# Moving the degree stores, the biases, the g row products and two Wv sums in the opening of a two-layer graph kernel

## The chip, the cores and the metric

The kernel runs on one core of one Trainium2 chip. The metric is the device time of one execution in microseconds (us); for a version it is the median of several runs. Everything is float32. The engines are PE (TensorE), DVE (VectorE), ACT (ScalarE), POOL (GpSimd) and SP (SyncE, which here only issues DMAs).

## The reference

64 graphs of 256 nodes with 512 features each, and a dense 256x256 adjacency per graph. Layer 0 is an attention masked by the adjacency, layer 1 a graph convolution, both on a layer-normed, rectified input and both with a residual:

```
h = relu(layernorm(x))
q, k, v = h @ Wq.T + bq, h @ Wk.T + bk, h @ Wv.T + bv
w = adj * exp(q @ k.T);  w = w / w.sum(-1)
x = x + w @ v
h = relu(layernorm(x))
A = adj + I;  d = A.sum(-1) ** -0.5
x = x + (A * d[:, None] * d[None, :]) @ (h @ W + b)
```

## The kernel before

**Tiling.** The graphs go in 32 pairs, p = 0 to 31. A pair's features are four blocks of 128 nodes x 512 (`TB` = 4), its adjacency four of 128 x 256. Every matrix product is done by a scheme of seven half-size products instead of eight, which needs sums and differences of the operands' quarters (`left_sums`, `right_steps`, `weight_steps`, suffixes S1 to S4). The stages of a pair are g (query-key product with the merged matrix M = Wq.T Wk, `query_stage`), v (values), s (scores and softmax), o (weights times values), l (neighbours' sum) and w (times W1); g1 is product 1 of stage g, and so on. PE runs the products in an order written out as a string of such tokens (L1113, L1144, L1153), one behind the other (`in_order`, L289). `work` lists the calls that follow each token on the other engines.

**Rounds.** The first `run` (L1112) does stages g, v and s of pair 0. Then round p does o, l, w of pair p and g, v, s of pair p + 1. Ahead of the first run lies the opening: PE runs ten products of a constant (`run_in`, L202), then M from Wq's and Wk's rows (`merge_query_key`, L208, 32 products of 128x256, two passes each), then 16 turns of pair 0's normed features (`transpose_features`, L410; ACT copies them out of PSUM at L419). PSUM has six buffers for all products.

**The other opening work.** `measure(p)` (L333) takes means and variances of the features of pair p on VectorE (L308, L309), and GpSimd turns them into scale and offset (L298, L300, L317, L319: `irs`, `irr`, `nm`, `nb`). `norm_features(p)` (L336) then applies them on ScalarE (L325). `degrees(p)` (L350) sums the adjacency's rows on VectorE (L353), takes the root on GpSimd and stores the 512 degrees from SP to DRAM, an element of 4 bytes at a time (`dflat`, L356). `spread_degrees(p)` (L359) loads them back as a row for all partitions (`drow`, L362); `weigh_degrees(p)` (L365, line L372) uses that row. `bias_products` (L248) computes bq.bk (`bb`, `bs`) and, through `weighted_rows` (L236), the rows g = sum of bq * Wk's rows: four multiplies on ScalarE and three adds on GpSimd (L243, L245). A second call (L1091) does c = sum of bk * Wq's rows, in the buffers with the tags "hbS" and "U2". `bias_terms` (L256, products `pc_gb`) and `query_row` (L266, product `c_all`) use them. `find_terms` (L393, line L398) needs `c_all`; `corner` (L643, line L646) reads stage g's products out of PSUM; `find_query_sums` (L478) is lines L436 to L439, `turn_blocks` (L404) line L408, `move` (L421) line L430; L785 is the first read of stage s's bank 1. Wv's quarters are turned at L273, and its four sums are L181 to L184 on VectorE; W1's four sums are the same lines on GpSimd.

**Order.** Within an engine instructions run in the order in which they stand; `tc.issue_after(x)` says that what is made within it stands behind x. [...] The biases bq and bk are loaded from GpSimd's queue (L131, L132), each as 128 x 4 elements of 4 bytes. Wk's three parts go from SP's queue and Wq's from ACT's (L136); behind Wk's on SP's queue follow pair 0's features (L101) and adjacency (L106), pair 1's features, Wv (L145), and then `load_the_rest` (L149), in whose middle `spread_degrees(0)` stands (L159). `degrees(0)` stores its row ahead of all of `load_the_rest`. `degrees(1)` follows token g2 (L1122), and Wv's sums follow g2 and g3.

Of the kernel before, what the change touches and what calls it, by code (L numbers as in the profile page):

```python
# [9 lines left out]
F32 = mybir.dt.float32  # L10
# [6 lines left out]
def kernel(  # L17
# [35 lines left out]
    nc = tc.nc  # L53
    P = 128
    B, N, D = x.shape
# [7 lines left out]
    DC = D // P  # L63
# [9 lines left out]
    p1 = ctx.enter_context(tc.tile_pool(name="p1", bufs=1))  # L73
# [7 lines left out]
    sub, add, mult = ALU.subtract, ALU.add, ALU.mult  # L81
# [7 lines left out]
    def load_x(p):  # L89

        x_tiles[p] = xp.tile([P, TB, D], F32, tag="x", name=f"x_{p}")
        for g in range(G):
            nc.sync.dma_start(of_graph(x_tiles[p], g), in_dram(x, p, g))
# [3 lines left out]
    def load_features(p):  # L97

        feats[p] = hp.tile([P, TB, D], F32, tag="h", name=f"h_a{p}")
        for g in range(G):  # L100
            nc.sync.dma_start(of_graph(feats[p], g), in_dram(x, p, g))  # L101
# [19 lines left out]
    wk_rows = p1.tile([P, DC, D], F32, tag="gT", name="wk_rows")  # L121
    wq_w1 = p1.tile([P, 7, 2, HD], F32, tag="yS", name="wq_w1")
    wq_rows = wq_w1[:, 0:DC].rearrange("p c h d -> p c (h d)")
# [4 lines left out]
    b_qk = const.tile([P, 2, DC], F32, tag="b_qk", name="b_qk")  # L128
    bqT, bkT = b_qk[:, 0], b_qk[:, 1]
    b1_all = const.tile([P, D], F32, tag="b1", name="b1_all")  # L130
    nc.gpsimd.dma_start(bqT, bq.rearrange("(c p) -> p c", p=P))  # L131
    nc.gpsimd.dma_start(bkT, bk.rearrange("(c p) -> p c", p=P))  # L132
    for first, count, half in ((0, 2, 0), (2, 2, 0), (0, 4, 1)):
        rows, cols = slice(first * P, (first + count) * P), ts(half, HD)
        for eng, tile_, w in ((nc.sync, wk_rows, wk), (nc.scalar, wq_rows, wq)):
            eng.dma_start(  # L136
                tile_[:, first : first + count, cols],
                w[rows, cols].rearrange("(c p) d -> p c d", p=P),
            )
    load_features(0)  # L140
    load_a(0)
    load_features(1)
# [6 lines left out]
    def load_the_rest():  # L149
        w1_view = w1.rearrange("(j t p) (i f) -> i j p t f", p=P, t=2, f=HD)  # L150
        nc.sync.dma_start(w1_set[:, A11], w1_view[0, 0])
        nc.sync.dma_start(w1_set[:, A12], w1_view[0, 1])
        nc.sync.dma_start(w1_21, w1_view[1, 0])
        nc.sync.dma_start(w1_set[:, A22], w1_view[1, 1])
        load_a(1)
        load_features(2)
        load_blocks(0)
        load_x(0)
        spread_degrees(0)  # L159
        load_x(1)  # L160
        nc.sync.dma_start(b1_all, b1.partition_broadcast(P))
# [10 lines left out]
    v_set = const.tile([P, 7, 2, HD], F32, tag="wv", name="v_set")  # L172
# [6 lines left out]
    def weight_steps(w, w21, eng=nc.vector):  # L179
        return [  # L180
            lambda: eng.tensor_tensor(w[:, S1], w21, w[:, A22], add),  # L181
            lambda: eng.tensor_tensor(w[:, S2], w[:, S1], w[:, A11], sub),
            lambda: eng.tensor_tensor(w[:, S3], w[:, A11], w21, sub),
            lambda: eng.tensor_tensor(w[:, S4], w[:, A12], w[:, S2], sub),  # L184
        ]
# [16 lines left out]
    def run_in():  # L202

        pm = ps_m.tile([P, P], F32, tag="pm", name="pm_run_in")
        for _ in range(10):
            in_order(pm, ones_sq, ones_sq, start=True, stop=True)

    def merge_query_key(behind_rows, behind_turns):  # L208


        m21 = p1.tile([P, 2, HD], F32, tag="A1", name="m21")
        for half, dcs in ((0, (0, 1)), (1, (0, 1)), (0, (2, 3)), (1, (2, 3))):
            pm = {
                dc: ps_m.tile([P, HD], F32, tag="pm", name=f"pm_mT_{dc}_{half}") for dc in dcs
            }
            for ocs in ((0, 1), (2, 3)):
                for dc in dcs:
                    for oc in ocs:
                        in_order(
                            pm[dc],  # L220
                            wq_rows[:, oc, ts(dc, P)],
                            wk_rows[:, oc, ts(half, HD)],
                            start=oc == 0,
                            stop=oc == DC - 1,
                        )
            for dc in dcs:
                to = half_of(m_set, m21, half, dc // 2)[:, dc % 2, :]
                if dc < 2 or half == 0:
                    with tc.issue_after(behind_rows):
                        behind_rows = nc.scalar.copy(to, pm[dc]).ins  # L230
                else:
                    with tc.issue_after(behind_turns):
                        behind_turns = nc.vector.tensor_copy(to, pm[dc]).ins
        return weight_steps(m_set, m21), behind_rows, behind_turns

    def weighted_rows(w, b, three, one, behind=None):  # L236

        more = p1.tile([P, DC - 1, D], F32, tag=three, name=f"wr_{three}")
        acc = p1.tile([P, D], F32, tag=one, name=f"wr_{one}")
        parts_ = [acc] + [more[:, i] for i in range(DC - 1)]  # L240
        for oc in range(DC):
            with tc.issue_after(behind) if behind else ExitStack():
                last = nc.scalar.mul(parts_[oc], w[:, oc, :], b[:, oc : oc + 1])  # L243
        for oc in range(1, DC):
            added = nc.gpsimd.tensor_tensor(acc, acc, parts_[oc], add)  # L245
        return acc, last.ins, added.ins

    def bias_products():  # L248
        bb = const.tile([P, DC], F32, tag="bb", name="bb")
        nc.vector.tensor_tensor(bb, bqT, bkT, mult)  # L250
        bs = const.tile([P, 1], F32, tag="bs", name="bs")
        nc.vector.tensor_reduce(bs, bb, AX.X, add)
        return bs, *weighted_rows(wk_rows, bqT, "vS", "A0")


    def bias_terms(bs, g_rows):  # L256
# [9 lines left out]
    def query_row(c_rows):  # L266
        in_order(c_all, ones_sq, c_rows, start=True, stop=True)

    v21 = p1.tile([P, 2, HD], F32, tag="wS", name="v21")

    def value_weight_steps():
# [9 lines left out]
    norms, deg, ds, terms, blocks, hTs, parts, second, sides = ({} for _ in range(9))  # L281
    flats, gTs, query_parts, weights, row_sums, turned, wTs, weight_parts, value_parts, aTs = (
        {} for _ in range(10)
    )

    measured, offsets = [], []
# [8 lines left out]
    def inverse_root(src, plus, name, tag="ir_r"):  # L295

        s = sm.tile([P, TB], F32, tag="ir_s", name=f"irs_{name}")
        nc.gpsimd.tensor_scalar(s, src, plus, None, add)  # L298
        r = sm.tile([P, TB], F32, tag=tag, name=f"irr_{name}")
        nc.gpsimd.tensor_tensor(r, s, minus_half, ALU.pow)  # L300
        return r
# [48 lines left out]
    def degrees(p):  # L350

        sums = sm.tile([P, TB], F32, tag="deg", name=f"deg_{p}")
        measured.append(nc.vector.tensor_reduce(sums, a_tiles[p], AX.X, add).ins)  # L353
        d = inverse_root(sums, 1.0, f"d{p}", "d")
        flats[p] = dr.tile([NT], F32, tag="drow", name=f"dflat_{p}")
        nc.sync.dma_start(flats[p].rearrange("(t p) -> p t", p=P), d)  # L356
        deg[p] = d, None

    def spread_degrees(p):  # L359

        row = p1.tile([P, NT], F32, tag="drow", name=f"drow_{p}")
        nc.sync.dma_start(row, flats[p].partition_broadcast(P))  # L362
        deg[p] = deg[p][0], row
# [719 lines left out]
        return work  # L1083

    run_in()
    bs, g_rows, last_act, last_pool = bias_products()
    with tc.issue_after(last_pool):
        measure(0)
    first_offsets = offsets[-1]
    with tc.issue_after(first_offsets):  # L1090
        c_rows, turned_rows, last_pool = weighted_rows(wq_rows, bkT, "hbS", "U2", last_act)  # L1091
    with tc.issue_after(measured[-1]), tc.issue_after(last_pool):
        degrees(0)
        with tc.issue_after(measured[-1]):
            measure(1)
    m_steps, last_act, last_dve = merge_query_key(turned_rows, measured[-1])
    load_the_rest()
    with tc.issue_after(last_act):
        norm_features(0)
# [4 lines left out]
        + value_weight_steps(),  # L1104
        last_dve,
    )
    v_steps = weight_steps(v_set, v21)
    with tc.issue_after(offsets[-1]):
        weight_sums(w1_set, w1_21, nc.gpsimd)
    behind = ExitStack()  # L1110
# [8 lines left out]
        {  # L1119
            "g1": [(norm_features, 1)],  # L1120
            "g6": [(lambda p: bias_terms(bs, g_rows), 0)],
            "g2": [(lambda p: query_row(c_rows), 0), (degrees, 1), (lambda p: [s() for s in v_steps[:2]], 0)],  # L1122
            "g7": [(find_terms, 0)],
            "g3": [(find_query_sums, 0), (turn_blocks, 1), (lambda p: [s() for s in v_steps[2:]], 0)],
            "v5": [(move, 1, 0, 6, nc.gpsimd)],
            "v6": [(move, 1, 6, 8)],
            "s1": [(move, 1, 8, 12)],
# [2 lines left out]
            "v2": [(move_weights, 0, 0, 8)],  # L1130
            "v3": [
                (turn_adjacency, 0),
                (weigh_degrees, 0),
                (spread_degrees, 1),
                (measure, 2),
# [14 lines left out]
    p = NP - 2  # L1150
# [74 lines left out]
```

## Time and profile before

| | us |
|---|---|
| median of the runs | 1806.53 |
| lowest and highest of the runs | 1805.68, 1808.04 |
| the profiled execution | 1807.14 |
| its span, from the first to the last instruction | 1805.0 |
| PE busy in the span | 1784.7 |
| VectorE, ScalarE, GpSimd busy | 1327.4, 1162.8, 1204.8 |
| granted TensorE clock, mean over the span | 0.998 |

All times in what follows count from the span's start. A line of the timeline has the start, the duration, the engine, the line of the kernel, the operation, what is written and read, and in brackets the engine's idle time before it and what ended that. "SPq" is a DMA issue by SP. A line of the waits has the total in us, the number of times and the longest. A matmul in float32 counts as two in the profile.

### The profile page before, as it was taken

Reading aid. Unit: us, or ns where it says so; the run is one execution under the profiler, and the core shown is the slowest. Engines: PE = TensorE matmul, PEld = TensorE weight load, DVE = VectorE, ACT = ScalarE, POOL = GpSimd, SP = SyncE. Lnnn points to the kernel's source line nnn. Section 1 sums busy time; section 2 is a strip of 40 time slices with the busy share of each in tenths; the row PEclk is TensorE's granted clock in tenths of the full one; section 3 lists DMA queues with packets and bytes.
Section 4 is the critical chain, followed back from the end, with each engine's and each line's share of the span. In section 5 each row is a group of like instructions: output and inputs, shape, how many; then the busy total and the mean of one; then the engine's idle time right before and its main releaser. Section 6 shows DMA issues by size and latency. Waiting matters only on the chain.

```text
span 1805.0 us, 29095 instructions
## 1 busy us (share of the span) xinstructions
PE 1784.7 (99%) x9968; PEld 1614.2 (89%) x9968; DVE 1327.4 (74%) x3054; ACT 1162.8 (64%) x2318; POOL 1204.8 (67%) x1326
## 2 busy tenths in 40 slices
PE   8999999999999999999999999999999999999998
PEld 7889988999989999989999889999899999899987
DVE  5877878777777677777678786777776777776676
ACT  4676667766677666677666767666776666776542
POOL 4467676676666676666676766776666766667763
PEclk9999999999999999999999999999999999999999
DMA  8634443544533444444444434444434444333331
GB/s 194 151 88 100 112 106 83 117 80 108 120 87 98 113 86 111 111 83 112 100 98 113 96 90 119 77 111 113 92 101 106 94 111 112 83 111 71 65 76 47
DMA packets 253603, 182.58 MB, mean 101 GB/s; under 512 B 163728, under 2 KB 184208, under 8 KB 253456
## 3 DMA queue, kind: packets, MB, share of 16 engines
q1 hardware_dynamic: 235424, 146.11, 28.7%
q0 software_dynamic: 16960, 33.56, 13.6%
q8 instruction: 80, 1.31, 0.3%
q10 hardware_dynamic: 1072, 1.05, 0.2%
q14 instruction: 67, 0.55, 0.1%
HBM read 147.07 MB, written 33.62 MB: 100 GB/s over the span
## 4 chain that ended last, share of the span: by engine, by line
PE 93%; DVE 3%; DMA 1%; ACT 1%; POOL 1%; issue 1%; SPq 0%; DVEq 0%; ACTq 0%; POOLq 0%
PE pm_g L292 21%; PE pm_w L292 21%; PE pm_v L292 20%; PE pm_s L292 10%; PE pm_o L292 10%; PE pm_l L292 10%; DMA a<-in_adj_dram 1%; DMA wk_rows<-in_L_gnn_Wk_w_dram 0%; ACT h_b L325 0%; DVE st_b L308 0%; POOL wr_U L245 0%; DVE e L774 0%; POOL wr_A L245 0%; ACT e L764 0%; DVE x L838 0%
## 5 line engine op out<-in xcount | busy, mean ns | idle before, releaser
L292 PE MATMUL pm_w<-w_set,yS 128*128 128x256 f32 x1792 | 399.1, 380 | 1.7 <-ACT U_w L922 1.3
L292 PEld LDWEIGHTS pm_w<-w_set,yS 128*128 128x128 f32 x1792 | 335.4, 190 | 45.3 <-issue 1.4
L430 ACT COPY hT<-hq 32x512 f32<-32x512 f32 x490 | 301.9, 616 | 10.2 <-DVE hq L408 2.7
L292 PE MATMUL pm_g<-hT,m_set 128*128 128x256 f32 x1024 | 239.0, 381 | 5.9 <-DVE gT L646 5.0
L292 PE MATMUL pm_v<-v_set,hT 128*128 128x256 f32 x1024 | 237.0, 379 | 0.1
L913 DVE SCALAR_TENSOR_TENSOR x<-pm_w,irr_d,x 128x256 f32<-128x256 f32 x256 | 110.8, 474 | 164.7 <-POOL x L923 114.8
L292 PEld LDWEIGHTS pm_g<-hT,m_set 128*128 128x128 f32 x1024 | 195.3, 191 | 34.0 <-DVE gT L646 5.4
L292 PEld LDWEIGHTS pm_v<-v_set,hT 128*128 128x128 f32 x1024 | 192.0, 190 | 25.6 <-DVE v L725 0.9
L512 ACT COPY wT<-eq 32x256 f32<-32x256 f32 x504 | 202.3, 401 | 5.9
L292 PE MATMUL pm_v<-v_set,hS 128*128 128x256 f32 x768 | 176.6, 380 | 0.0
L292 PE MATMUL pm_g<-hS,m_set 128*128 128x256 f32 x768 | 176.3, 379 | 0.2 <-DVE hS L449 0.2
L292 PEld LDWEIGHTS pm_g<-hS,m_set 128*128 128x128 f32 x768 | 145.8, 190 | 20.4 <-DVE hS L449 0.6
L292 PEld LDWEIGHTS pm_v<-v_set,hS 128*128 128x128 f32 x768 | 144.0, 191 | 18.5
L838 POOL TENSOR_TENSOR x<-x,A_o 128x512 f32<-128x512 f32 x62 | 82.0, 1324 | 111.4 <-ACT A_o L836 108.2
L764 ACT ACTIVATE e<-e,ks 128x128 f32<-128x128 f32 x192 | 66.5, 395 | 83.9 <-DVE e L802 43.5
L946 POOL TENSOR_TENSOR yS<-yS,U_l 128x512 f32<-128x512 f32 x32 | 40.7, 1272 | 118.6 <-DVE yS L945 114.8
L325 ACT ACTIVATE h_b<-x,nb_b,rs_b 128x512 f32<-128x512 f32 x128 | 93.7, 802 | 18.8 <-POOL nb_b L319 18.8
L292 PE MATMUL pm_l<-aT,h_b 128*128 128x128 f32 x776 | 102.9, 275 | 2.5 <-DVE U_l L936 2.2
L292 PE MATMUL pm_s<-hT,gT 128*128 128x128 f32 x768 | 101.3, 275 | 3.5 <-DVE e L785 3.5
L292 PEld LDWEIGHTS pm_s<-hT,gT 128*128 128x128 f32 x768 | 97.9, 192 | 7.4 <-DVE e L785 4.3
L832 DVE TENSOR_TENSOR x<-pm_o,x 128x512 f32<-128x512 f32 x128 | 87.6, 686 | 17.7 <-PE pm_o L292 17.1
L436 POOL TENSOR_TENSOR wS<-wT 128x256 f32<-128x256 f32 x32 | 23.4, 730 | 115.5 <-ACT wT L512 115.5
(182 smaller groups left out, 3938.2 us busy)
## 6 DMA issues: line engine op xcount, KB each, us to landing
h_a<-in_x_dram SPq DMA_DIRECT2D x64, 512.0 KB, 7.1
x<-in_x_dram SPq DMA_DIRECT2D x64, 512.0 KB, 4.4
x<-in_L_gnn_Wv_b_dram POOLq DMA_DIRECT2D x32, 1024.0 KB, 10.2
out_dram<-x SPq DMA_DIRECT2D x62, 512.0 KB, 3.5
a<-in_adj_dram SPq DMA_DIRECT2D x64, 256.0 KB, 2.9
aq<-in_adj_dram SPq DMA_DIRECT2D x128, 128.0 KB, 3.6
drow<-dflat SPq DMA_DIRECT2D x32, 256.0 KB, 5.9
wv_blocks<-in_L_gnn_Wv_w_dram SPq DMA_DIRECT2D x4, 256.0 KB, 6.8
```

The lines of the kernel that those rows point to most:

```text
L292: last_product[0] = nc.tensor.matmul(*args, **kwargs).ins
L325: nc.scalar.activation(h[:, t, :], xt[:, t, :], AF.Relu, bias=nb[:, t : t + 1], scale=rd[:, t : t + 1],)
L430: copy(dst[j * Q : (j + 1) * Q, i], src[i * Q : (i + 1) * Q, j])
L436: eng.tensor_tensor(s1, a21, a22, add)
L512: copy(dst[j * Q : (j + 1) * Q, i], src[i * Q : (i + 1) * Q, j])
L764: nc.scalar.activation(block(qb, kb)[:, g], scores[:, g], AF.Exp, bias=terms[p][:, t : t + 1])
L832: read(nc.vector.tensor_tensor(block(n, i), bank, block(n, i), add))
L838: read(eng.tensor_tensor(block(n, i), block(n, i), more, add))
L913: nc.vector.scalar_tensor_tensor(to, bank[:, r, :], factor(n, r), to, mult, add)
L946: read(nc.gpsimd.tensor_tensor(t2, b22, t["part"], sub))
```

## The change

- The loads of bq and bk leave GpSimd's queue: bq goes to SP's queue behind Wk's three parts and ahead of the features, bk to ACT's queue behind Wq's three parts.
- `run_in` has eight products instead of ten.
- g is computed on VectorE alone (one multiply, three multiply-and-adds of 128x512). c alone is left to `weighted_rows`; its buffers are now "hbS" and "aS".
- `degrees` no longer stores for pair 0; a new function `flatten` does, and for pair 0 it is called in `load_the_rest` behind `load_x(0)`.
- `degrees(1)` moves from token g2 to token v3, the last of the first run, behind `turn_adjacency(0)`.
- Wv's sums S1 and S2 stay on VectorE, S3 and S4 go to GpSimd; all four are made behind g2.

```diff
-    nc.gpsimd.dma_start(bqT, bq.rearrange("(c p) -> p c", p=P))
-    nc.gpsimd.dma_start(bkT, bk.rearrange("(c p) -> p c", p=P))
     for first, count, half in ((0, 2, 0), (2, 2, 0), (0, 4, 1)):
...
+    nc.sync.dma_start(bqT, bq.rearrange("(c p) -> p c", p=P))
+    nc.scalar.dma_start(bkT, bk.rearrange("(c p) -> p c", p=P))
     load_features(0)
...
         load_x(0)
+        flatten(0)
         spread_degrees(0)
         load_x(1)
...
-        for _ in range(10):
+        for _ in range(8):
...
-    def weighted_rows(w, b, three, one, behind=None):
+    def weighted_rows(w, b):
-        more = p1.tile([P, DC - 1, D], F32, tag=three, name=f"wr_{three}")
-        acc = p1.tile([P, D], F32, tag=one, name=f"wr_{one}")
+        more = p1.tile([P, DC - 1, D], F32, tag="hbS", name="wr_more")
+        acc = p1.tile([P, D], F32, tag="aS", name="wr_acc")
...
-        return bs, *weighted_rows(wk_rows, bqT, "vS", "A0")
+        g_rows = p1.tile([P, D], F32, tag="A0", name="g_rows")
+        nc.vector.tensor_scalar(g_rows, wk_rows[:, 0, :], bqT[:, 0:1], None, mult)
+        for oc in range(1, DC):
+            last = nc.vector.scalar_tensor_tensor(
+                g_rows, wk_rows[:, oc, :], bqT[:, oc : oc + 1], g_rows, mult, add
+            )
+        return bs, g_rows, last.ins
...
-        d = inverse_root(sums, 1.0, f"d{p}", "d")
+        deg[p] = inverse_root(sums, 1.0, f"d{p}", "d"), None
+        if p:
+            flatten(p)
+
+    def flatten(p):
         flats[p] = dr.tile([NT], F32, tag="drow", name=f"dflat_{p}")
-        nc.sync.dma_start(flats[p].rearrange("(t p) -> p t", p=P), d)
-        deg[p] = d, None
+        nc.sync.dma_start(flats[p].rearrange("(t p) -> p t", p=P), deg[p][0])
...
-    bs, g_rows, last_act, last_pool = bias_products()
-    with tc.issue_after(last_pool):
+    bs, g_rows, last_dve = bias_products()
+    c_rows, last_act, last_pool = weighted_rows(wq_rows, bkT)
+    with tc.issue_after(last_dve), tc.issue_after(last_pool):
         measure(0)
-    first_offsets = offsets[-1]
-    with tc.issue_after(first_offsets):
-        c_rows, turned_rows, last_pool = weighted_rows(wq_rows, bkT, "hbS", "U2", last_act)
-    with tc.issue_after(measured[-1]), tc.issue_after(last_pool):
+    with tc.issue_after(measured[-1]), tc.issue_after(offsets[-1]):
         degrees(0)
...
-    v_steps = weight_steps(v_set, v21)
+    v_steps = weight_steps(v_set, v21)[:2] + weight_steps(v_set, v21, nc.gpsimd)[2:]
...
-            "g2": [(lambda p: query_row(c_rows), 0), (degrees, 1), (lambda p: [s() for s in v_steps[:2]], 0)],
+            "g2": [(lambda p: query_row(c_rows), 0), (lambda p: [s() for s in v_steps], 0)],
...
-            "g3": [(find_query_sums, 0), (turn_blocks, 1), (lambda p: [s() for s in v_steps[2:]], 0)],
+            "g3": [(find_query_sums, 0), (turn_blocks, 1)],
...
                 (turn_adjacency, 0),
+                (degrees, 1),
                 (weigh_degrees, 0),
```

In the order in which the changed kernel's instructions then stand, `bb` is VectorE's first operation on data, and g's four follow it ahead of `measure(0)`; ScalarE's table load and its four multiplies wait for bk and all of Wq, and GpSimd's three adds stand ahead of `irs_a`; on GpSimd the sum S3 of Wv stands ahead of W1's four sums and S4 behind them; the root of pair 1's degrees stands between the first two of the sums `wS` (L436, L437 on GpSimd).

More of the change, by code (lines that the diff above doesn't have):

```diff
@@ L234, in merge_query_key @@
         return weight_steps(m_set, m21), behind_rows, behind_turns
-    def weighted_rows(w, b, three, one, behind=None):
-        more = p1.tile([P, DC - 1, D], F32, tag=three, name=f"wr_{three}")
-        acc = p1.tile([P, D], F32, tag=one, name=f"wr_{one}")
+    def weighted_rows(w, b):
+        more = p1.tile([P, DC - 1, D], F32, tag="hbS", name="wr_more")
+        acc = p1.tile([P, D], F32, tag="aS", name="wr_acc")
         parts_ = [acc] + [more[:, i] for i in range(DC - 1)]
         for oc in range(DC):
-            with tc.issue_after(behind) if behind else ExitStack():
-                last = nc.scalar.mul(parts_[oc], w[:, oc, :], b[:, oc : oc + 1])
+            last = nc.scalar.mul(parts_[oc], w[:, oc, :], b[:, oc : oc + 1])
         for oc in range(1, DC):
@@ L1095 @@
             measure(1)
-    m_steps, last_act, last_dve = merge_query_key(turned_rows, measured[-1])
+    m_steps, last_act, last_dve = merge_query_key(last_act, measured[-1])
     load_the_rest()
```

## The prediction, on record before the changed kernel was run

> **What bounds the kernel now.** I read the page first: does one engine fill the span?
>
> ```profile
> PE 1784.7 (99%) x9968; PEld 1614.2 (89%) x9968; DVE 1327.4 (74%) x3054; ACT 1162.8 (64%) x2318; POOL 1204.8 (67%) x1326
> ```
>
> PE is busy 1784.7 of 1805.0 us, and a full round takes 54.86 us (round 1's last products begin at 168.16, round 2's at 223.02) with nothing idle in it. An edit of the opening can therefore gain or lose only what it changes in PE's idle time there; what PE is early or late at the first full round, it carries to the end. Second view: what PE waits for in the first 86 us (total, times, longest).
>
> ```profile
> PE pm_g L292 <- DVE gT L646: 5.0, 1, 5.0
> PE pm_s L292 <- DVE e L785: 2.1, 1, 2.1
> PE pm_run_in L292 <- DVE ones_sq L164: 1.0, 1, 1.0
> PE pm_g L292 <- ACT U_g L660: 0.7, 1, 0.7
> PE pm_g L292 <- ACT hT L419: 0.3, 1, 0.3
> ```
>
> Third view: the timeline around the 5.0. VectorE sits at degrees(1)'s sum (L353) until graph pair 1's adjacency lands, and the L646 read that frees g3's PSUM bank stands behind it.
>
> ```profile
> 24.79 0.38 SPq L356 DMA_DIRECT2D dflat<-irr_d  x1
> ...
> 41.38 1.22 DVE L353 TENSOR_REDUCE deg<-a 128x4 f32<-128x1024 f32 x1 [5.03 <-DMA a<-in_adj_dram]
> ...
> 43.05 3.78 PE L292 MATMUL pm_g<-hT,m_set 128*128 128x256 f32 x8 [4.98 <-DVE gT L646]
> ```
>
> g3's eight passes take 3.78 us, and eight of the same kind 1.89 at 36.18. The table of windows says why (length, PE busy, PEld, DVE, ACT, POOL, then granted clock):
>
> ```profile
> 36.95:40.35 3.40, 1.12 (x6) 0.64 (x4) 0.00 (x0) 0.85 (x3) 1.16 (x1) 1.00 1.08 371
> 40.36:43.77 3.41, 0.72 (x2) 0.64 (x3) 2.35 (x5) 0.00 (x0) 3.25 (x4) 0.50 1.16 324
> 43.77:47.18 3.41, 3.41 (x10) 2.69 (x9) 1.56 (x5) 0.00 (x0) 1.83 (x3) 0.50 0.84 107
> 54.00:57.40 3.40, 2.14 (x19) 2.14 (x20) 2.06 (x4) 3.02 (x5) 3.19 (x6) 1.00 1.23 212
> ```
>
> The stall halves the clock up to 47.18, so it costs another 1.9 us. Why does the adjacency land only at 41.29? The DMA view of 25 to 36 us: issued are dflat (512 stores of 4 bytes) and, behind it on SP's queue, 2 MB of loads.
>
> ```profile
> DMA packets 759, 0.23 MB, mean 21 GB/s; under 512 B 538, under 2 KB 759, under 8 KB 759
> ...
> dflat<-irr_d SPq DMA_DIRECT2D x1, 2.0 KB, 11.3
> ```
>
> The 4-byte store takes 11.3 us to land, and the loads behind it crawl at 21 GB/s.
>
> **The change, part by part** (us in the profiled execution; g1 to g7 are the seven query products).
>
> *Stall, clock, U_g: gains.* degrees(1) leaves VectorE's queue ahead of L646: minus 4.98. The clock then holds: g3 in 1.89 instead of 3.78, minus 1.9. Without the early dflat, W1 (1 MB) and the adjacency (0.5 MB) follow Wv's landing at 25.35 at some 350 GB/s, so the latter lands near 30 instead of 41.29: this gain is covered twice. c_rows leaves the buffer "U2", which u2's copy shares (ACT waits 1.45 for c_all's product), so g7's wait of 0.68 goes.
>
> *Two sums of Wv to GpSimd: a gain.* After g3 the next PE wait is 2.1 on L785. VectorE's chain to it (L398, L646, L436 to L439, L408) ends with L183 and L184, 0.57 and 1.02: minus 1.55 from that chain. On GpSimd they cost 1.27 each (the row of L181 there), in its waits of 11.6 and 7.7. Price: GpSimd's sums now run beside VectorE's S1 and S2; a 128x512 add took 1.65 beside GpSimd's adds at 21.62 and 0.68 alone, so 0 to 1.9, of which about 1 is slack before g3. I take plus 0.3 (0 to 0.9).
>
> *Biases: the loss.* Before, they land at 8.5 and 9.56 on a queue of their own. Now bq stands behind Wk on SP's queue, ahead of features and adjacency, and bk behind Wq on ACT's. Call T the time when bk and all of Wq are there. Everything in front hangs on T: `bb` heads VectorE's queue, and behind it stand g_rows and measure(0), which GpSimd awaits; ACT's table load and four Wq multiplies start at T, then GpSimd's three adds, then nb_a, the norm, the turns, g1. Before, the same chain ran from Wk's landing (in the chain of waits):
>
> ```profile
> 1.74 7.92 DMA wk_rows<-in_L_gnn_Wk_w_dram
> ...
> 9.75 1.28 ACT L243
> 11.04 0.72 ACT wr_A L243
> 11.77 0.62 ACT wr_vS L243
> 12.39 0.07 issue
> 12.46 0.58 POOL wr_A L245
> ```
>
> Its start is 9.70, the norm's 18.41; g1 (22.35, already waiting 0.28 for ACT) follows. So g1 moves by T minus 9.70. Wq's last part landed at 12.46. What is T? In 6 to 9 us the two biases, 1024 elements of 4 bytes, took 41.9% of 16 engines:
>
> ```profile
> q0 software_dynamic: 63, 0.00, 41.9%
> q1 hardware_dynamic: 293, 0.33, 34.2%
> q10 hardware_dynamic: 251, 0.26, 24.3%
> ```
>
> That is 1.26 us, 0.6 each, about 20 ns an element; gone from in front of the weights it lets Wq land near 11.2 or a little before. At best bk needs no more time than the earlier Wq: T = 10.8. In 9 to 11 us ACT's queue moved 247 packets beside SP's 294, about one for one; if each of bk's 32 elements per engine waits for a 2048-byte feature packet (85 ns), 32 x 105 ns = 3.3: T = 14.5. I take 12.8, near the middle. [...]
>
> g1: 22.35 + 3.1 = 25.45; g5 at its end, 27.2 instead of 24.52: plus 2.7. g_rows on VectorE (one of at most 0.6, three of 0.68, as L398) ends at T + 2.9, measure(0) at T + 5.9, under GpSimd's adds (to T + 6.8); measure(1), the copies and m_set's sums follow, and hS is ready at T + 13.6 = 26.4, under g1's end. Both covers are about 0.8; without them each microsecond costs one. Two run-in products fewer (0.85 us) cost nothing and bring nothing: the first weights landed at 3.98 and 4.28, the run-in would end at 4.6, and PE then waits for the norm.
>
> *degrees(1) at the round's end: a loss.* VectorE is busy all 9.0 us of 66 to 75 and 10.86 of the next 11; 1.22 more pushes all behind it. g3 at 79.17 needs an L646 that ended at 78.14 (slack 1.03): 0.2. v5 at 86.08 needs the bank of an L646 that ended at 84.94, now behind three transposes: 0.4. The wait at 100.69 (1.41, on ACT, fed by VectorE) can grow by 0.5. Sum 1.1 (0 to 2.4). GpSimd's two root steps, 1.3 between its wS sums, end by 76.6; the product that reads them last runs at 80.9.
>
> *What is late next.* ACT's six moves of hT (3.75) now end about 1 after the scores are ready, and v3 already waited 0.51 on what follows: plus 0.5. dflat(0) now delays only x(1), drow(0) and b1: landed near 55, wanted near 60.
>
> **Sum.** g3 starts at 43.05 - 4.98 - 0.68 + 2.7 = 40.1; L785 releases s7 at g3's start + 12.2 - 1.9 - 1.5 = 8.8, at 48.9 instead of 55.26: minus 6.4. Then + 0.5 + 1.1 + 0.3: **minus 4.5**. The profiled execution took 1807.14 (span 1805.0 and 2.14 around it), 0.6 over the runs' median; 1802.6 for it, and for the median 1806.53 - 4.5 = **1802.0**.
>
> **Rivals.** 0.2% is 3.6 us, about what a measurement of this kernel can tell from no change.
> 1. *bk costs nothing* (T = 10.8): 2.0 less, 1800.0. For it: 20 ns an element. Against: one-for-one service. 0.20.
> 2. *The losses at their upper ends*: degrees(1) 2.4, ports 0.9: 1.9 more, 1803.9; with T = 14.5, 1805.6. For it: VectorE's full windows. Here too a cold front: PE idles about 1.8 for ACT's copies of mT and 1.3 for the norm; a window one third busy lost the clock (36.95), one 63% busy (54.00) did not. Half clock costs up to 3.4, half of it under waits: 1.7. [...] 0.17.
> 3. *4-byte loads hold the queue as the 4-byte store does* (slower). bq lies ahead of the features; at dflat's rate both biases land about 10.5 behind the weights, T = 20.2: 7.4 more, and 1.7 for a cold clock: minus 4.5 becomes plus 4.6, 1811.1. It decides from T = 17.3 on. For it: 11.3 us for 2 KB. Against: the same bias loads took 1.26 us of the engines. 0.10.
> 4. *The stall only changes its name*: g3 waits as long on something else, and the front's loss eats the rest: 1806.5. Against: VectorE's other work ahead of L646 is 0.7. 0.05.
>
> The forecast has 0.48. Faster by over 0.2% (under 1802.9): three quarters of it, 0.36, rival 1, and 0.04 of rival 2: 0.60. Slower: rival 3, 0.10. Within: 0.30. Range: the unknown terms' ends give 8.4 and 0.9 less, 1798.1 and 1805.6; 1798.5 to 1806.0 leaves out rival 3 and half of rival 4.
>
> **What would show it.** Right: L353 behind the adjacency's transposes; g3 in 1.9 at clock 1.00, starting near 40; L243 starting at 12 to 13.5; g1 near 25.5. Wrong: b_qk landing after 17 (rival 3); PEclk 0.50 after 10 us; PE waits over 1.5 on L646 between 66 and 86.

## The result and the profile after

The changed kernel takes 1799.78 us (median of 5 runs, 1799.14 to 1800.94); the kernel before takes 1806.98 beside it (5 runs, 1805.68 to 1808.04). The ratio is 0.9962, 95% interval 0.9947 to 0.9976: 7.2 us less, where 4.5 was forecast. The profiled execution took 1800.09, its span 1798.1 instead of 1805.0. (Of run 1 below only the times without a profile are used: its profiled execution ran at a mean granted clock of 0.556.)

First the page, as before: PE fills the span in the same way.

```profile
PE 1783.0 (99%) x9964; PEld 1612.5 (90%) x9964; DVE 1328.9 (74%) x3056; ACT 1160.7 (65%) x2314; POOL 1200.4 (67%) x1323
```

PE was busy 1.7 us less: g3 and v5 at full clock and two run-in products fewer make 3.0, and groups in which another engine sets the pace give some of it back (the norm's turns, 0.7 more). The other 5.2 of the span's 6.9 are idle time. So the second view again, PE's waits in the first 86 us (total, times, longest).

```profile
PE pt_h L426 <- ACT h_a L331: 1.6, 1, 1.6
PE pm_run_in L298 <- DVE ones_sq L165: 1.0, 1, 1.0
PE pm_v L298 <- DVE v L734: 0.7, 1, 0.7
PE pm_s L298 <- DVE e L794: 0.7, 1, 0.7
PE pm_g L298 <- ACT hT L428: 0.3, 1, 0.3
```

The 5.0 for L646 (now L655) is gone, the wait for L785 (now L794) fell from 2.1 to 0.7, the 0.7 for U_g is gone. New are 1.6 for the norm, at the head of the list, and 0.7 for L734. Third, the timeline of PE: g3 has no wait in brackets and takes 1.89.

```profile
38.73 1.89 PE L298 MATMUL pm_g<-hT,m_set 128*128 128x256 f32 x8
40.45 3.62 PE L298 MATMUL pm_v<-v_set,hS 128*128 128x256 f32 x16
...
47.44 0.82 PE L298 MATMUL pm_s<-hT,gT 128*128 128x128 f32 x5 [0.69 <-DVE e L794]
```

The table of windows (length, PE busy, PEld, DVE, ACT, POOL, granted clock, then DMA share and GB/s) shows PE busy throughout and no 0.50 in the slices of the old stall:

```profile
36.95:40.35 3.40, 3.40 (x17) 2.98 (x17) 3.33 (x7) 1.43 (x3) 1.87 (x2) 1.00 1.00 216
40.36:43.77 3.41, 3.41 (x18) 3.00 (x17) 3.31 (x10) 0.00 (x0) 0.00 (x0) 1.00 1.35 281
```

And the DMA view of 25 to 36 us: 246 GB/s instead of 21, no 4-byte store among the issues; the adjacency of pair 1 lands at 31.78 instead of 41.29.

```profile
DMA packets 3997, 2.71 MB, mean 246 GB/s; under 512 B 2136, under 2 KB 3483, under 8 KB 3995
```

**Where the time went.** I took the start of each of PE's groups in both traces and subtracted. A change of that difference is a gain or a loss at that place:

| PE group | before | after | difference | what happened there |
|---|---|---|---|---|
| turns `pt_h` | 20.16 | 21.50 | +1.33 | PE waits 1.6 for the norm |
| g1 | 22.35 | 24.56 | +2.21 | ACT's copies of the turns follow it |
| g5 | 24.52 | 26.39 | +1.87 | |
| g7 | 32.62 | 33.55 | +0.93 | wait for U_g gone |
| g3 | 43.05 | 38.73 | -4.32 | stall gone |
| v5 | 46.62 | 40.45 | -6.17 | full clock |
| s7 | 55.26 | 47.44 | -7.83 | Wv's two sums left the chain |
| v3 | 64.39 | 57.19 | -7.20 | starts 2.62 behind the group before it instead of 2.00 (wait for L734) |
| o1, round 0 | 74.85 | 67.92 | -6.94 | ACT's moves of wT, 0.3 later |
| g1, round 1 | 123.47 | 117.19 | -6.27 | PE waits 0.6 for L945 at 101.17 |

From there the difference stays at -6.2 to PE's end; the last 0.7 of the span lies behind the last VectorE operation, in the closing stores.

### The profile page after: what moved, and what is told of

It is laid out like the page before. It is cut to its first block, busy times and chain, and to the rows that moved or that the text cites. A ratio compares the mean times of both kernels' runs of the same rounds, so it can differ in the third digit from the quotient of the medians.

```text
span 1798.1 us, 29084 instructions
## 1 busy us (share of the span) xinstructions
PE 1783.0 (99%) x9964; PEld 1612.5 (90%) x9964; DVE 1328.9 (74%) x3056; ACT 1160.7 (65%) x2314; POOL 1200.4 (67%) x1323
## 4 chain that ended last, share of the span: by engine, by line
PE 92%; DVE 4%; DMA 1%; ACT 1%; issue 1%; POOL 0%; ACTq 0%; DVEq 0%; POOLq 0%
PE pm_g L298 21%; PE pm_w L298 21%; PE pm_v L298 20%; PE pm_l L298 10%; PE pm_s L298 10%; PE pm_o L298 10%; DMA b_qk<-in_L_gnn_Wk_b_dram 1%; DVE st_a L314 0%; DMA dflat<-irr_d 0%; DMA drow<-dflat 0%; ACT hT L439 0%; ACT h_b L331 0%; DVE e L783 0%; DVE st_b L314 0%; ACT e L773 0%
```

## The experiments

Twelve kernels were run. "After" edits start from the changed kernel, "before" edits from the kernel before. The times are medians; each stands beside the kernel before on the same chip. A few tenths are not to be read from the times (one kernel's runs spread over up to 3.3 us), so the verdicts rest on the PE starts of the traces. A trace is of one execution each, and its span belongs to that execution, not to the median.

| run | kernel | time | before beside it | ratio, 95% interval | span |
|---|---|---|---|---|---|
| 1 | after, degrees(1) at g2 | 1800.41 | 1807.99 | 0.9942 to 0.9972 | - |
| 2 | after, dflat(0) early | 1800.73 | 1807.99 | 0.9946 to 0.9976 | 1798.6 |
| 3 | after, both | 1801.67 | 1807.99 | 0.9950 to 0.9977 | 1799.8 |
| 4 | before, degrees(1) at v3 | 1804.25 | 1807.99 | 0.9972 to 0.9991 | 1802.2 |
| 5 | after, biases on GpSimd | 1801.60 | 1806.58 | 0.9963 to 0.9984 | 1799.5 |
| 6 | after, biases ahead of the weights' last half | 1800.75 | 1806.58 | 0.9956 to 0.9979 | 1798.0 |
| 7 | after, front in another order | 1798.10 | 1806.58 | 0.9938 to 0.9968 | 1796.1 |
| 8 | after, S3 and S4 on VectorE | 1800.51 | 1806.58 | 0.9960 to 0.9982 | 1797.7 |
| 9 | before, degrees(1) at v3, dflat(0) late | 1801.24 | 1806.74 | 0.9957 to 0.9980 | 1800.4 |
| 10 | before, PE filled ahead of g3 | 1806.67 | 1806.74 | 0.9990 to 1.0008 | 1804.3 |
| 11 | before, biases alone moved | 1806.56 | 1806.74 | 0.9990 to 1.0008 | 1805.0 |
| 12 | run 7 and two more steps | 1798.13 | 1806.74 | 0.9934 to 0.9964 | 1794.9 |

### Is the stall's gain covered twice? Runs 1, 2 and 3

```diff
-            "g2": [(lambda p: query_row(c_rows), 0), (lambda p: [s() for s in v_steps], 0)],
+            "g2": [(lambda p: query_row(c_rows), 0), (degrees, 1), (lambda p: [s() for s in v_steps], 0)],
...
-                (degrees, 1),
```

> The kernel after, with degrees(1) put back behind the query product g2, so ahead of L646 on VectorE; dflat(0) stays late. Theory (the stall's gain is covered twice, since the adjacency of graph pair 1 now lands at 31.8 us instead of 41.3): VectorE sits 1.2 us in the sum at about 34 and waits for nothing; g3 starts within 1 us of 38.73, the clock holds, the time is 1800 plus or minus 1.5. Rival (only the place of degrees(1) took the stall away): g3 waits on L646 again by several us, the clock falls to 0.50, the time is 1804 to 1807.

1800.41, as the theory has it; what VectorE and PE did is not shown by a trace here.

```diff
     def degrees(p):
...
-        if p:
-            flatten(p)
+        flatten(p)
...
-        flatten(0)
         spread_degrees(0)
```

> The kernel after, with dflat(0) stored from degrees(0) again, ahead of the loads on SP's queue; degrees(1) stays behind v3. Theory (covered twice): the adjacency of pair 1 lands near 40 again, but nothing on VectorE ahead of L646 reads it; g3 starts within 0.5 us of 38.73 and the time is 1800 plus or minus 1.5. Rival (the late loads are needed elsewhere): W1, the adjacency or the blocks of aq0 and x(0), 10 us later, give a new wait of PE and 1 to 5 us back.

The adjacency landed at 38.52 and nothing ahead of g3 waited for it; g3 kept its place within 0.2. s7 waits 0.5 longer, and PE ends 0.5 later. As the theory has it.

> The kernel after, with both undone: degrees(1) behind g2 and dflat(0) ahead of the loads. Theory: VectorE waits for the adjacency until about 40 to 41, L646 ends near 42.5 and g3 starts near 43, where it started before, at clock 0.50 to 47: the stall is as long as before plus what g3 was early (4.3), and the clock's 1.9 is lost too; time 1805 to 1807. Rival (the two are worth what each alone brings, under 1 us): 1800 to 1801.5.

The edit is both of the above. Here my theory fell. g3 starts at 40.12, not at 43, and waits only 0.7:

```profile
PE pm_g L297 <- DVE gT L653: 0.7, 1, 0.7
```

So there is a third cover beside the two that the prediction named. SP's issue and the DMA view show the third cover:

```profile
21.57 0.99 SPq L364 DMA_DIRECT2D dflat<-irr_d  x1
```

```profile
DMA packets 1587, 1.77 MB, mean 161 GB/s; under 512 B 90, under 2 KB 1374, under 8 KB 1586
```

The store is issued at 21.57 instead of 24.79 and lands at 30.75 instead of 36.09, so the adjacency lands at 35.82. Before, GpSimd made Wq's three adds (18.33 to 22.7) between the offsets and pair 0's root, which the store reads; after, those adds stand ahead of the offsets and the root starts at 20.18 instead of 22.68. Moving Wk's rows off GpSimd thus freed the store, and with it the loads behind it, while the front's loss moved VectorE's need for them later: the sum of the adjacency starts at 38.47 without a wait. How much of the cover is the earlier store and how much the later need, this run does not separate.

### Each part on the kernel before: runs 4, 9 and 11

Run 4 is one part alone:

```diff
-            "g2": [(lambda p: query_row(c_rows), 0), (degrees, 1), (lambda p: [s() for s in v_steps[:2]], 0)],
+            "g2": [(lambda p: query_row(c_rows), 0), (lambda p: [s() for s in v_steps[:2]], 0)],
...
                 (turn_adjacency, 0),
+                (degrees, 1),
```

> The kernel before with one part of the change alone: degrees(1) at v3, behind the turns of the adjacency. dflat(0), the biases, Wk's rows and the sums of Wv stay as before. Theory (this part alone takes the stall and the lost clock, and the front is untouched): g3 starts near 43.05 - 4.98 = 38.1 (or up to 0.7 later, where it still waits for U_g), at clock 1.00; time 1807 - 4.3 to 6.9 = 1800 to 1802.7. Rival (the stall changes its name because the loads are as late as before): g3 waits on something else, time over 1804.

g3 starts at 38.09, 4.96 earlier, and v5 6.80 earlier: the stall and the clock, as worked out. Then most of it goes again: s7 is 4.94 earlier, o1 3.0. PE waits (the view of waits, first 125 us) now for L785:

```profile
PE pm_s L292 <- DVE e L785: 5.4, 2, 4.0
```

The timeline shows why. W1 still lands late, so GpSimd's four sums of it run beside VectorE's L437 and L438, which take 1.13 and 1.75 (0.65 and 0.68 in the kernel before):

```profile
42.04 1.68 POOL L182 TENSOR_TENSOR w_set<-w_set 128x512 f32<-128x512 f32 x1
...
43.14 1.13 DVE L437 TENSOR_TENSOR gS<-gS,gT 128x512 f32<-128x512 f32 x1
...
43.80 1.59 POOL L184 TENSOR_TENSOR w_set<-w_set 128x512 f32<-128x512 f32 x1
44.19 1.75 DVE L438 TENSOR_TENSOR gT<-gT 128x512 f32<-128x512 f32 x1
...
48.28 0.64 DVE L183 TENSOR_TENSOR v_set<-v_set,v 128x512 f32<-128x512 f32 x1
48.41 3.94 POOL L430 COPY hT<-hq 32x512 f32<-32x512 f32 x5 [3.02 <-DVE hq L408]
48.85 1.09 DVE L184 TENSOR_TENSOR v_set<-v_set 128x512 f32<-128x512 f32 x1
49.86 0.41 DVE L785 TENSOR_TENSOR e<-pm_s,e 128x256 f32<-128x256 f32 x1
```

and the idle PE loses the clock again, one place later (columns as above):

```profile
47.07:50.48 3.41, 0.15 (x1) 0.15 (x2) 3.20 (x6) 2.06 (x4) 1.98 (x3) 1.00 0.88 254
50.48:53.89 3.41, 3.41 (x17) 3.41 (x18) 0.85 (x2) 1.63 (x3) 3.29 (x5) 0.50 0.98 293
```

So the rival that the stall changes its name holds for half of the gain, when this part is made alone.

Run 9 adds the late store to run 4:

```diff
+        if p:
+            flatten(p)
...
         load_x(0)
+        flatten(0)
         spread_degrees(0)
```

> The kernel before with two parts of the change: degrees(1) at v3 and dflat(0) stored behind the loads. The last-but-one look (degrees(1) at v3 alone) gained 5.0 at g3 and 1.9 by the clock, and lost 3.5 of it before s7, where PE waited 4.0 for L785: GpSimd's sums of W1 ran from 39.5 to 45.4 beside VectorE's L437 and L438 (1.13 and 1.75 us instead of 0.65 and 0.68). Theory (W1's late landing, 40.1, is what moved those sums there): with dflat late, W1 lands near 30, the sums run before 38, L437 and L438 take 0.7 again, s7 comes 1.5 earlier than there and the clock holds through it; time 1800 to 1801.5. Rival (VectorE's chain with Wv's two sums is the bound whatever GpSimd does): PE's wait for L785 stays near 4 and the time near 1804.

L437 and L438 take 0.65 and 0.68, the wait is 2.3, s7 comes at 48.74: the theory's half about GpSimd is right. The clock did not hold in the profiled execution: PE was busy a third of the window ahead, and ran at half clock in the next. This is not so each time: four of the seven runs have a mean clock of 1.000 and take 1800.33 to 1801.24, the other three 0.999 and 1801.77 to 1802.87 (the profiled one took 1802.52).

```profile
46.05:49.46 3.41, 1.10 (x10) 0.91 (x9) 2.63 (x5) 2.62 (x5) 2.55 (x3) 1.00 0.63 153
49.46:52.87 3.41, 3.41 (x18) 3.41 (x18) 0.85 (x2) 1.96 (x6) 3.16 (x5) 0.50 0.43 55
```

Run 11 moves the two loads of biases alone:

```diff
-    nc.gpsimd.dma_start(bqT, bq.rearrange("(c p) -> p c", p=P))
-    nc.gpsimd.dma_start(bkT, bk.rearrange("(c p) -> p c", p=P))
...
+    nc.sync.dma_start(bqT, bq.rearrange("(c p) -> p c", p=P))
+    nc.scalar.dma_start(bkT, bk.rearrange("(c p) -> p c", p=P))
     load_features(0)
```

> The kernel before, with the two biases alone moved to the weights' queues, behind Wk and Wq. The prediction's step (the biases are the front's whole loss, because the chain in front hangs on the landing of bk) would have g1 2.2 later. Theory now: the first rows are Wk's here, and need Wk (8.8) and bq (10.1) alone, so ACT's multiplies start 0.4 later than 9.70, g1 at 22.4 to 22.9 instead of 22.35, and the time is 1807 plus or minus 0.8. Rival (VectorE's bb, which needs bk at 11.9 and stands ahead of measure(0), holds the norm): g1 1 to 1.5 later, time 1808 to 1808.5.

ACT's table load starts at 9.87 with bq's landing, `bb` at 11.32 with bk's, and g1 starts at 22.45 (+0.10); the time is the same. The place of the biases costs the kernel before nothing.

### What holds the front: runs 5, 6 and 7

Run 5 puts the biases' two loads back on GpSimd's queue in the kernel after (the lines of run 11's edit, turned round).

> The kernel after, with the two biases back on GpSimd's queue, issued first. Theory A (the biases' place is the front's whole loss): they land near 9, ACT's multiplies start near 9.7, g1 is 2.2 us earlier than in the kernel after (24.56 to 22.4) and the time is near 1797.6. Theory B (the order of the rows is the loss: ahead of the norm now stand Wq's rows, not Wk's, and Wq's last part comes later beside the biases' 1024 small elements): ACT's multiplies start when Wq is there, at 11.5 to 12.5; g1 is 24 to 25.2, the time 1799.4 to 1800.4.

Theory B, by the trace; the time of 1801.60 is above the range of either theory. The biases land at 8.34 and 9.65, but Wq's last part only at 12.55 beside them (9.13 in the kernel after), ACT starts at 12.64 and g1 at 25.38, 0.82 **later**. Moving the biases was a gain of some 0.7 for this order of rows, not the loss. A half-clocked window (23.04 to 26.45) adds 0.4, so that g5 is 1.26 later. The run also shows which engine holds the norm here: VectorE, with both biases early, gives the variances at 15.61, and GpSimd's offsets still start only behind its three adds of Wq's rows.

```profile
15.31 0.30 DVE L315 BATCH_NORM_AGGREGATE mv_a<-st_a 128x2 f32<-128x6 f32 x2
...
19.41 0.24 POOL L304 TENSOR_SCALAR irs_a<-mv_a 128x4 f32<-128x4 f32 x1
```

```diff
     for first, count, half in ((0, 2, 0), (2, 2, 0), (0, 4, 1)):
+        if half:
+            nc.sync.dma_start(bqT, bq.rearrange("(c p) -> p c", p=P))
+            nc.scalar.dma_start(bkT, bk.rearrange("(c p) -> p c", p=P))
...
-    nc.sync.dma_start(bqT, bq.rearrange("(c p) -> p c", p=P))
-    nc.scalar.dma_start(bkT, bk.rearrange("(c p) -> p c", p=P))
```

Run 6 is this edit.

> The kernel after, with bq and bk issued ahead of the last half of Wk and of Wq on the same two queues, so no features beside bk. Theory (bk's 2.75 us behind Wq are spent beside the packets of the features): bk and Wq are both there at 9.7 to 10.7, ACT's multiplies start then, g1 1 to 2 us earlier than 24.56, the time 1798 to 1799. Rival (the small elements only push Wq back by as much): start 11.5 to 12, time as after, 1799.8 plus or minus 0.7.

Nearly the rival: the biases land at 6.98 and 8.12, Wq at 11.18 instead of 9.13, ACT starts at 11.28 instead of 11.98, and g1 is 0.32 earlier. With the small elements ahead of it Wq's last part lands 2.05 later; behind it, in the kernel after, bk had landed 2.75 later. But g1 is held by PE here: Wk's last part lands at 10.29, PE waits 2.0 for it and runs the next window (11.53 to 14.95) at half clock, so M is ready only at 22.48 and the turns follow without a wait. The norm itself starts 0.71 earlier than in the kernel after (19.92 instead of 20.63), so what that is worth this run does not show.

```diff
-        bb = const.tile([P, DC], F32, tag="bb", name="bb")
-        nc.vector.tensor_tensor(bb, bqT, bkT, mult)
...
         g_rows = p1.tile([P, D], F32, tag="A0", name="g_rows")
...
+        bb = const.tile([P, DC], F32, tag="bb", name="bb")
+        with tc.issue_after(last.ins):
+            nc.vector.tensor_tensor(bb, bqT, bkT, mult)
...
-    c_rows, last_act, last_pool = weighted_rows(wq_rows, bkT)
-    with tc.issue_after(last_dve), tc.issue_after(last_pool):
+    with tc.issue_after(last_dve):
         measure(0)
+    c_rows, last_act = weighted_rows(wq_rows, bkT, offsets[-1])
```

This is run 7; `weighted_rows` puts its adds behind its third argument.

> The kernel after, with the front in another order and no transfer changed: VectorE does Wk's rows first (they need bq alone, there at 10.1), bb and bs behind them, and GpSimd's three sums of Wq's rows stand behind the offsets of measure(0) instead of ahead of it. Theory (the norm waits for GpSimd, 3.2 us of nb_a, because those sums hold it, and VectorE's chain waits for bk at 11.9): nb_a is ready near 18.5 instead of 20.39, VectorE's chain to hS 1.5 to 1.8 earlier, g1 at 22.6 to 23.2 instead of 24.56, the time 1797.8 to 1798.6. Rival (ACT or the turns bound g1 anyway): g1 within 0.4 of 24.56, time as after. A second rival: c_all's product waits for the sums of Wq's rows, which end near 23 now, and costs what g1 gains; it stands at about 31, so I do not expect it.

As the theory has it, and more. In the kernel after GpSimd's adds hold the offsets until 18.76, though VectorE gave the variances at 17.57 (the timeline; the last line is ACT's norm):

```profile
11.91 0.16 DVE L250 TENSOR_TENSOR bb<-b_qk 128x4 f32<-128x4 f32 x1 [10.91 <-DMA b_qk<-in_L_gnn_Wk_b_dram]
...
14.69 3.99 POOL L245 TENSOR_TENSOR wr_acc<-wr_acc,wr_more 128x512 f32<-128x512 f32 x3 [13.38 <-ACT wr_more L243]
...
17.27 0.30 DVE L315 BATCH_NORM_AGGREGATE mv_a<-st_a 128x2 f32<-128x6 f32 x2
...
18.76 0.23 POOL L304 TENSOR_SCALAR irs_a<-mv_a 128x4 f32<-128x4 f32 x1
...
20.63 0.81 ACT L331 ACTIVATE h_a<-h_a,nb_a,irr_a 128x512 f32<-128x512 f32 x1 [3.18 <-POOL nb_a L325]
```

In run 7 nothing stands in their way:

```profile
9.83 0.49 DVE L251 TENSOR_SCALAR g_rows<-wk_rows,b_qk 128x512 f32<-128x512 f32 x1 [8.84 <-DMA b_qk<-in_L_gnn_Wq_b_dram]
...
15.76 0.23 POOL L306 TENSOR_SCALAR irs_a<-mv_a 128x4 f32<-128x4 f32 x1 [14.45 <-DVE mv_a L317]
...
17.63 1.52 ACT L333 ACTIVATE h_a<-h_a,nb_a,irr_a 128x512 f32<-128x512 f32 x2 [0.68 <-POOL nb_a L327]
```

g1 starts at 21.56, 3.0 earlier than after and 0.8 earlier than before; 2.1 of it remain at `pc_gb`. The run changes two orders at once, and neither was tried alone. By the rows, GpSimd's adds in the way are worth 1.2 of the 3.0 (18.76 against variances at 17.57), and VectorE's start with bq instead of bk the other 1.8 (variances at 15.67). Without the first the second brings nothing: in run 5 VectorE was as early, and GpSimd still held the offsets.

### Wv's two sums, the clock, and a better version: runs 8, 10 and 12

Run 8 gives S3 and S4 back to VectorE, behind g3's reads:

```diff
-    v_steps = weight_steps(v_set, v21)[:2] + weight_steps(v_set, v21, nc.gpsimd)[2:]
+    v_steps = weight_steps(v_set, v21)
...
+            "g3": [(find_query_sums, 0), (turn_blocks, 1), (lambda p: [s() for s in v_steps[2:]], 0)],
```

> The kernel after, with S3 and S4 of Wv's sums back on VectorE behind g3's reads. Theory (they stood in the chain to L785): PE's wait for L785 grows from 0.69 to about 2.2, all behind it is 1.3 to 1.6 later, time 1801.1 to 1801.5. Rival (GpSimd's sums cost VectorE's S1 and S2 as much beside them, 1.33 and 1.59 instead of 0.68): S1 and S2 come back to 0.7, g3 is up to 1 earlier, and the time is 1799.8 plus or minus 0.7.

At s7 the theory: its wait is 2.3, and the difference to the kernel after goes from -0.81 (bk landed 0.8 earlier there, by chance) to +0.81, so 1.62. But at v3 only +0.19 is left and after 101 us -0.49: the waits of 0.7 for L734 and 0.6 for L945 are not there. Of the 1.62 the kernel keeps 0.3 (-0.49 against the -0.81 at the start). That holds for this execution, the shortest of seven: four take 1799.83 to 1800.51 at a mean clock of 1.000, and three take 1802.63 to 1803.10 at 0.998. The trace has a window with PE 49% busy ahead of s7 that kept the clock; a window lost there would cost more, but no trace of the longer executions is on record.

Run 10 puts products of ones by ones into the stall of the kernel before, into a bank that nothing uses yet.

```diff
+    def fill(p):
+        for _ in range(34):
+            in_order(b1_row[:, 0:P], ones_sq, ones_sq, start=True, stop=True)
...
+            "g4": [(fill, 0)],
```

> The kernel before, with 34 products of 128x128 put into PE's stall ahead of g3 (ones by ones into a bank that nothing uses yet; nothing else is changed and they end before g3 can start). Theory (the clock fell because PE was idle, and cost 1.9 on g3 and nothing else that lasts): g3 starts at 43.05 as before, at granted clock 1.00, takes 1.89, and all behind it is 1.9 earlier; time 1804.9 to 1805.5. Rival 1 (VectorE bounds s7, so PE's faster g3 only waits longer there): the gain is under 0.5. Rival 2 (the clock falls all the same): no gain.

The filler was twice too long: 68 passes in 7.75 us, so that g3 started at 45.54, 2.5 late, against my expectation. It ran at clock 1.00 in 1.89, and s7 started at 55.13, 0.13 earlier than before. The run doesn't isolate the clock; what it shows is that g3 could start 2.5 later at full clock at no cost, because VectorE's chain from g3's end sets s7; VectorE also did its fourth L398 in the longer wait, so that its chain behind g3 was 0.7 shorter.

Run 12 starts from run 7. One of Wq's adds goes ahead of the offsets, and the copy of b into PSUM from among ACT's moves of wT to token o2 of round 0.

```diff
+    c_rows, last_act, adds = weighted_rows(wq_rows, bkT)
+    first_add = adds[0]()
+    with tc.issue_after(last_dve), tc.issue_after(first_add):
         measure(0)
+    for step in adds[1:]:
+        with tc.issue_after(offsets[-1]):
+            step()
...
+            work["o2"] = [(lambda p: nc.scalar.copy(b1_row, b1_all), 0)] + work.get("o2", [])
```

> The kernel with the front in the better order (Wk's rows on VectorE first, measure(0)'s offsets ahead of Wq's sums on GpSimd), and two more steps: one of the three sums stands ahead of measure(0)'s offsets, where GpSimd waits for VectorE, so that none runs beside VectorE's first sum for m_set (L182, 1.77 us beside them, 0.69 without); and the copy of b into PSUM stands behind the first output products instead of among ACT's moves of wT. Theory: hS 1.1 earlier, g5's wait of 0.6 for it gone, 0.3 from ACT's moves: 0.6 to 0.9 less than 1798.1, so 1797.2 to 1797.5. Rival (a later wait takes it back, as the waits for U_l took 0.6 in the kernel after): 1798 plus or minus 0.4.

g5 no longer waits for hS and is 3.02 ahead of the kernel after (2.25 in run 7), o1 3.31, so the 0.3 of ACT's moves is back. In round 1 a wait takes part of it back (view of waits, 125 to 200 us; the kernel after has none there):

```profile
PE pm_l L301 <- DVE U_l L948: 0.6, 1, 0.6
```

The difference stays at 3.2 in the profiled execution, which was the shortest of four; the other three have spans of 1796.0 to 1796.5, where run 7's four have 1796.1 to 1796.5. By its time, 1798.13 (1796.75 to 1798.37), the rival's figure, run 12 can't be told from run 7. They are 8.5 and 8.6 us shorter than the kernel before beside them, where the kernel after is 7.2 shorter; the intervals of these ratios overlap, so that the two also beat the kernel after rests on the traces (spans of 1796.1 and 1794.9 against 1798.1).

## Why the prediction was right or wrong

- **Stall and clock: right.** From g7 to g3 the difference moves by 5.25 where 4.98 was worked out, and to v5 by a further 1.85 where it was 1.9. "Covered twice" was an undercount (run 3), and "the stall changes its name" was underrated: made alone on the kernel before, the move gives 3.7 of 6.9 (run 4).
- **The front: the right chain, too narrow a cause, the wrong size.** ACT's rows start when bk and all of Wq are there, and g1 moved by T minus 9.70: 11.91 - 9.70 = 2.21 (and in run 8, where bk landed earlier, 11.08 - 9.70 = 1.38 with g1 1.40 later than before). T was mis-sized, 12.8 taken, 11.9 measured, and that it came so near was luck: Wq, put near 11.2, landed at 9.13, and bk, put 1.6 behind it, landed 2.75 behind. The name, "Biases: the loss", says too little. Run 11 moves them at no cost, and run 5 puts them back at a loss. What makes bk's landing count is the new order: the rows ahead of the norm are now Wq's, which need bk, instead of Wk's, with their adds ahead of the offsets on GpSimd, and VectorE's first operation, `bb`, needs bk too. Run 7 undoes both and has 3.0 back with every transfer where it was. g5 lost 1.87 instead of 2.7.
- **U_g: right.** 0.9 against 0.68. With T and the stall's 0.3 this put g3 at 38.73 instead of 40.1: 1.4 of the 2.4 us by which the sum missed.
- **Wv's sums: right at its place, wrong as a gain of the kernel.** 1.55 worked out, 1.62 measured at s7; 0.3 remain in run 8's trace, which is of its shortest execution. Its price on GpSimd's side, 0.3, was nothing at PE: L182 and L183 took 1.33 and 1.59, ahead of g3 by enough slack.
- **ACT's moves: right**, 0.6 against 0.5 at v3.
- **degrees(1) at the round's end: the step that failed.** 1.1 was put on it, and PE lost nothing there: from o1 to the product at 100.11 the difference stays at -6.94, and the wait of 1.41 at 99.28 is 1.41 at 92.34. VectorE did run its sum ahead of the rest, but was only about 0.4 later relative to PE, as its four L381 operations (L372 before) took 0.40 to 0.47 instead of 0.40 to 0.95, together 0.9 less. Later PE loses 0.6 on L945, where the mask L783 takes 1.42 beside a GpSimd sum instead of 0.43. That is not degrees(1): run 3, with it at g2, has the same wait, and run 8, with it at v3, has not. By these rows it comes and goes with which operations of the two engines meet.
- **Not foreseen:** the copy of b among ACT's moves (0.3, run 12).

The terms as measured: -7.83 at s7, +0.63 to v3, +0.26 to o1, +0.7 to round 1, and -0.7 behind PE's end, which I can't assign: -6.9 in the span. Rival 3 is out: both biases land by 11.88. Rival 1, a free bk, is out as well; that its time of 1800.0 came out near was luck: T was 0.9 under my value and degrees(1) cost nothing. The cold front of rival 2 did not happen in the kernel after, but did in runs 3, 5 and 6.

What stays open: why bk's few bytes take 2.75 behind Wq was not measured by itself, the two orders of run 7 were not tried one at a time, and the clock's 1.9 was not tried alone, as run 10's filler was too long.

## What to carry to other kernels

Gains in a chain of engines don't add: here the sum's place alone removed the stall on the kernel before (run 4, span 1802.2), and with the sum's and the store's places both undone in the kernel after 0.7 of it was left (run 3, 1799.8). And what an engine gains at one wait is given back at the next where another engine sets the pace. Ask of a step what it waits for *and* what its output holds up: the late load cost the front 2.2 only because three sums that need it stood ahead of a 1.8 us chain that everything needed, and VectorE's first operation waited for it too. And when an idle stretch goes, look at the windows of the clock behind the next wait before counting its gain (run 4: 0.50 behind a wait of 4.0).

## What the runs showed of the hardware

**The clock fell behind windows in which PE was busy up to 57% of the time.** In these traces the granted clock stood at 0.50 for one window of 3.41 us (run 9, 49.46 to 52.87) or two (before, 40.36 to 47.18), with 1.00 on both sides; where these windows begin differs from run to run (40.36 before and 11.53 in run 6, 8.45 windows apart). The next window was at half clock after windows in which PE was busy 0% (run 11), 4% (run 4), 32% (run 9), 33% (before), 42% (run 6), 49% (run 3), 51% (run 5) and 57% (run 11, at 1776); it stayed at 1.00 after 49% (run 8), 52% (run 2) and 59% (after). So in these runs a window in which PE was idle for 1.75 us was followed by half clock (run 3) and one in which it was idle for 1.73 was not (run 8); what decides between 49% and 57% is not shown. In run 11 the half-clocked window at 42.11, in which PE was busy 74%, was followed by a second one at half clock. Two windows beside each other, of run 3 (lost) and run 8 (kept), show how close the two outcomes lie:

```profile
19.27:22.68 3.41, 1.66 (x10) 0.99 (x10) 3.27 (x10) 2.43 (x4) 3.09 (x7) 1.00 1.58 133
22.68:26.10 3.42, 3.42 (x13) 2.77 (x13) 2.19 (x4) 2.42 (x5) 1.74 (x3) 0.50 1.48 131
```

```profile
44.26:47.67 3.41, 1.68 (x16) 1.48 (x14) 3.41 (x6) 1.65 (x4) 1.30 (x2) 1.00 0.79 107
47.67:51.09 3.42, 2.85 (x25) 2.85 (x26) 1.37 (x4) 3.05 (x7) 3.25 (x6) 1.00 0.56 110
```

And run 11's, the 74% at half clock and the 57% that lost it:

```profile
42.11:45.52 3.41, 2.54 (x6) 2.09 (x7) 2.81 (x8) 0.00 (x0) 3.25 (x4) 0.50 1.01 166
45.52:48.93 3.41, 3.41 (x9) 2.69 (x9) 2.13 (x6) 0.00 (x0) 0.18 (x1) 0.50 1.01 266
...
1776.08:1779.49 3.41, 1.93 (x11) 1.14 (x9) 0.69 (x2) 3.40 (x6) 0.00 (x0) 1.00 0.00 0
1779.49:1782.91 3.42, 3.28 (x8) 2.69 (x9) 3.42 (x6) 0.00 (x0) 1.27 (x1) 0.50 0.02 5
```

**Stores of single floats.** The 2 KB of dflat(0) took 9.2 to 11.5 us from issue to landing wherever it stood (24.79 to 36.09 before, 37.77 to 49.26 after, 21.57 to 30.75 in run 3), and large loads queued behind it on the same queue waited about as long (W1's parts a median of 12.5 from issue to landing before and 9.4 in run 3, against 5.6 in the kernel after); behind it in the kernel after stood only what is wanted late.
